# Layer 0's feed-forward spread between layer 1's attention steps, and two slot units of layer 3 begun in layer 2's scatter

## The chip, the cores and the metric

The kernel runs on one core of one Trainium2 chip. A core has five engines, each of which runs its own list of instructions in order: PE (matmuls and transposes), DVE (VectorE), ACT (ScalarE), POOL (GpSimd) and SP, which only issues DMAs here. An instruction waits until the semaphores that it names have been reached; what stands behind it on the same engine waits too. The metric is the time of one execution on the device, in microseconds. Before the change it is 901.73 us in the median of 14 runs (898.76 to 907.01).

## The reference

The input x is 16 sequences of 128 tokens of width 128, in float32. It goes through four layers; in each, a mixing step and a feed-forward add to x through a gate tanh(g). What matters here is this:

```python
x = x + tanh(g_xattn[0]) * L0_xattn(layernorm(x), ctx)      # 8 experts, each token goes to 2 of them, chosen by ctx
x = x + tanh(g_ffn[0])   * L0_ffn(layernorm(x))             # below
x = x + tanh(g_xattn[1]) * L1_xattn(layernorm(x), ctx, ctx) # 16 heads of 8, over blocks of 64 tokens
x = x + tanh(g_ffn[1])   * L1_ffn(layernorm(x))             # 8 linear maps, one chosen per output element
x = x + tanh(g_xattn[2]) * L2_xattn(..., hops)              # a gated memory; position rows picked by itok
x = x + tanh(g_ffn[2])   * L2_ffn(layernorm(x))             # experts choose tokens: gather, two products, scatter
x = x + tanh(g_xattn[3]) * L3_xattn(layernorm(x), ctx)      # slots: 3 rounds of attention and a GRU
x = x + tanh(g_ffn[3])   * L3_ffn(layernorm(x))             # weights rounded to -1, 0, 1

def L0_ffn(x):
    hq = float_quantize(relu(x @ w1.T + b1))                # 512 hidden, rounded to an 8-bit float
    return float_quantize(hq @ float_quantize(w2).T + float_quantize(b2))   # 16-bit float

def L3_xattn(slots, ctx):                                   # the slots are the 128 tokens of a sequence
    k, v = rmsnorm(ctx) @ Wk.T, rmsnorm(ctx) @ Wv.T
    for _ in range(3):
        attn = softmax(scale * (rmsnorm(slots) @ Wq.T) @ k.T, axis=slots)
        attn = attn / (attn.sum(over ctx) + eps)
        slots = gru(attn @ v, slots)
    return slots
```

The feed-forward of layer 0 and the norms work row by row, so each of the 16 sequences could go on by itself; layer 1's attention needs q from its own sequence alone, and k and v from ctx.

## The kernel before

x stays in on-chip memory as 16 tiles of 128 tokens by 128 (`k.x`). A "batch" is one such tile, a "chunk" four of them (BJ = 4, NJ = 4 chunks). The sub-layers are functions called in turn (`LAYERS`, L1721), and each is written as a pipeline over chunks, batches or blocks. What order an engine gets is set in two ways. In most sub-layers a planner orders the instructions, from its own estimate of durations and from what depends on what. In `l1_ffn`, `l2_ffn` and `l3_xattn`, `k.nc` is an `Engines` object (L51), which ties each instruction to the one before it on its engine (`InOrder`, L28), so that the order in the code is the order on the engine; this is called a told order.

*Layer 0.* `l0_xattn` (L284) sorts the tokens by expert into 39 blocks of 128 rows. A one-hot tile `of` serves to find the rows; then for each block GpSimd gathers the rows (`l_xs`, L454), SP loads the expert's first-layer weights (`l_w`, 258 KB each, into seven buffers in one tile of the tag w16a), PE computes, and the result goes to DRAM. `l0_returned(b)` (L503) brings the two expert outputs of each token of batch b back: two indirect DMAs on GpSimd (`l_back`, L512), each followed by an addition to x on VectorE (L519). Each gather is held behind the last addition but one (`k.behind`). `l0_ffn` (L545) issues the returns of chunk 0, then runs `pipeline(NJ, (hidden, 0), (output, 1))`: `hidden(j)` is the layer norm of chunk j (L197), four matmuls and relu into an 8-bit tile, and the two returns of a batch of the next chunk after each matmul; `output(j)` is 16 fp8 matmuls, the bias (L583) and the addition to x.

*Position gathers.* Layer 2 needs 65 gathers of position rows by indirect DMA on GpSimd (L961). They are spread: `k.gather(done)` issues the next one behind the instruction given. In layer 1's attention `maxima` and `normed` each issue one per batch. `turn_positions(n)` (L970) transposes four gathered tiles on PE and ACT copies them; six of these lie in `l0_ffn`, the others in `l1_ffn`.

*Layer 1's attention* (L595) is a pipeline over 16 batches with eight stages: queries, maxima, turned, weights, values, normed, output, projected. `project(j)` makes the norm, q and k of chunk j, and `project_values(j)` its v; `queries` calls project(0) first and project(j+1) at batch 4j+2. GpSimd masks q and k by head (L663, twice per batch) and the turned maxima (L703). PE's first product of batch b takes the masked k and is called kz(b) below.

*Layer 1's feed-forward* (L797) runs 64 small steps in a told order, with three of the next norms (`pieces`) in it.

*Layer 2's scatter and layer 3.* At the end of `l2_ffn`, 19 told steps (t in range(19)) scatter the 16 units' outputs back to x, and in them the layer norm and first root-mean-square norm of chunks 0 to 2 are made (`l3_first`, advanced by `more`). Layer 3's attention (L1466) has 12 units, 3 rounds by 4 chunks; its loop starts at t = 1 and unit u passes through the turn of its normed slots at t = u + 1 (g), scores and softmax at u + 2 (b), the weighted sum at u + 3 (c) and the gates' tanh and the new state at u + 4 (d). Chunk 3's first norms are advanced in t = 1 to 3.

Of the kernel before, what the change touches and what calls it, by code (L numbers as in the profile page):

```python
# [18 lines left out]
P = 128  # L19
# [31 lines left out]
class Engines:  # L51


    def __init__(self, tc, nc):
        self.nc = nc
        self.tensor, self.vector, self.scalar, self.gpsimd = (
            InOrder(tc, e) for e in (nc.tensor, nc.vector, nc.scalar, nc.gpsimd)
        )
# [5 lines left out]
class Kernel:  # L64
# [29 lines left out]
    def w2k(self, name):  # L94
        return self.work.tile([P, 512], F32, tag="w2k", name=name, bufs=13)
# [101 lines left out]
    def norm(self, j, keep=None, twice=False, pow=None):  # L197


        nc = self.nc  # L200
        st = self.sm([P, BJ, 6], "ln_st")
        mv = self.sm([P, BJ, 2], "ln_mv")
        for i in range(BJ):
            nc.vector.bn_stats(st[:, i, :], self.x[:, BJ * j + i, :])
            nc.vector.bn_aggr(mv[:, i, :], st[:, i, :])
        rs = self.sm([P, BJ], "ln_rs")
        if pow is None:
            self.rsqrt(rs, mv[:, :, 1], 1e-5)
        else:
            nc.vector.tensor_scalar(rs, mv[:, :, 1], 1e-5, None, ALU.add)  # L210
            nc.gpsimd.tensor_tensor(rs, rs, pow, ALU.pow)
        yield
        xn = keep if keep is not None else self.w2k("xn").rearrange("p (b d) -> p b d", b=BJ)
        for i in range(BJ):
            nc.vector.tensor_scalar(
                xn[:, i, :], self.x[:, BJ * j + i, :], mv[:, i, 0:1], rs[:, i : i + 1], ALU.subtract, ALU.mult
            )
# [75 lines left out]
def l0_xattn(k):  # L293
# [94 lines left out]
    of = k.work.tile([P, 2 * NB, 2, NBLK], BF16, tag="l0_of", name="l0_of", bufs=1)  # L388
# [117 lines left out]
def l0_returned(k, b):  # L506
# [3 lines left out]
    for i in range(2):  # L510
# [5 lines left out]
        if len(k.l0_added) > 1:  # L516
            k.behind(dma, k.l0_added[-2])
# [26 lines left out]
def l0_ffn(k):  # L544
# [11 lines left out]
    k.l0_added = []  # L556
    l2_gates_of_ctx(k)
    for b in range(BJ):
        l0_returned(k, b)

    def hidden(j):
        k.layernorm(j)
        hq = k.work.tile([P, NF, N], FP8, tag="w4k", name="l0f_q", bufs=3)
        for f in range(NF):
# [3 lines left out]
            if j + 1 < NJ:  # L568
                l0_returned(k, BJ * (j + 1) + f)
            if j and f % 2:  # L570
                turn_positions(k, 2 * (j - 1) + f // 2)
        return hq

    def output(j, hq):
# [7 lines left out]
        y = k.work.tile([P, N], F16, tag="w2k", name="l0f_y", bufs=13)  # L582
# [6 lines left out]
    pipeline(NJ, (hidden, 0), (output, 1))  # L589
# [3 lines left out]
def l1_xattn(k):  # L593
# [9 lines left out]
    k.banks(bank=8)  # L603
# [6 lines left out]
    nc.gpsimd.memset(neg, -1.0)  # L610
    for g in range(G):
        rows = neg[32 * g : 32 * g + 32, :]
        nc.gpsimd.affine_select(
            out=rows, in_=rows, pattern=[[-2, 4]], compare_op=ALU.is_ge, fill=0.0, base=0, channel_multiplier=1
        )
        nc.gpsimd.affine_select(
# [18 lines left out]
    for v in vs:  # L635
        nc.gpsimd.memset(v, 0.0)
        nc.gpsimd.memset(v[0:64, :, :, DH : DH + 1], 1.0)
        nc.gpsimd.memset(v[64:P, :, :, 2 * DH + 1 : 2 * DH + 2], 1.0)
    qkT = {}

    def project(j):
        k.layernorm(j)
# [27 lines left out]
    def queries(b):  # L670
        if b == 0:
            project(0)
            project_values(0)
        if b % BJ == 2 and b // BJ + 1 < NJ:
            project(b // BJ + 1)
        if b % BJ == 3 and b // BJ + 1 < NJ:

            project_values(b // BJ + 1)
        return masked(b)

    def maxima(b, qk):
# [11 lines left out]
        k.gather(done)  # L693
# [85 lines left out]
    for t in range(NB + 6):  # L779
        for fn, lag in stages:  # L780
            b = t - lag
            if 0 <= b < NB:
                args = (state.pop((after[fn], b)),) if fn in after else ()
                state[fn, b] = fn(b, *args)
        if t == NB + 1:

            xn = k.work.tile([P, BJ, P], F32, tag="w4k", name="l1f_xn", bufs=3)
            k.layernorm(0, keep=xn, pow=k.half)

def l1_ffn(k):
# [105 lines left out]
    for s in range(C * NJ + 24):  # L898
# [35 lines left out]
        if s % 2 and s // 2 <= P // 8 - 6:  # L934
            turn_positions(k, s // 2 + 6)
        for n in pieces.get(s, []):
            if n not in under_way:
                under_way[n] = k.norm(n[1], pow=k.half)
# [288 lines left out]
def l2_ffn(k):  # L1227
# [10 lines left out]
    k.l3_pool = k.l3_stack.enter_context(k.tc.tile_pool(name="l3_in", bufs=1, side="right"))  # L1238
    stack = ExitStack()
# [145 lines left out]
    k.l3_more = more  # L1385
    for t in range(NB + 3):
# [6 lines left out]
        more()  # L1393
        if t % BJ == 2 and t > 2:
# [71 lines left out]
def l3_xattn(k):  # L1466

# [54 lines left out]
    def weights(u, s, m):  # L1522
        rs = k.l3_rs[:, BJ * (u % NJ) : BJ * (u % NJ + 1)]
        tot, e = k.sm([P, BJ], "l3_tot"), w2k("l3_e")
# [7 lines left out]
    def weighted(u, tot):  # L1532
# [4 lines left out]
        v = pool.tile([P, BJ, P + 1], F32, tag="l3_vs", name="l3_vs")  # L1537
# [43 lines left out]
    sn, snT, at, ups, pg, sq = k.l3_first, {}, {}, {}, {}, {}  # L1581
    ffn = k.l3_ffn
    hs, norms = {}, {j: ffn.normed(j) for j in range(NJ)}
    for t in range(1, U + 4):
        a, g, b, c, d = (t - lag if 0 <= t - lag < U else None for lag in range(5))
        out = t - U - 1
        if t == NJ - 1:
# [29 lines left out]
        if t < NJ:  # L1617
# [98 lines left out]
LAYERS = [l0_xattn, l0_ffn, l1_xattn, l1_ffn, l2_xattn, l2_ffn, l3_xattn]  # L1716
# [86 lines left out]
```

## Time and profile before

| | us |
|---|---|
| median of 14 runs | 901.73 |
| profiled execution, its own time | 901.9 |
| span of the profiled execution | 900.2 |
| busy: PE / DVE / ACT / POOL | 728.2 / 515.4 / 402.0 / 421.5 |
| mean granted clock of PE | 0.909 |
| last block of layer 0's experts ends | 131.2 |
| feed-forward of layer 0, to its last fp8 matmul | 131.5 to 201.8 |
| layer 1's attention, first kz to the last stage | 210.28 to 340.87 |
| last norm's transposes in the scatter | 739.61 |

The profile is one execution. Its page gives the busy share of each engine in 40 slices of the span (22.5 us each; a digit is tenths), the chain of work that ended last, and groups of instructions. The trace behind it answers questions: a window's busy times, one line's instructions and whom they wait for, a chain of waits in a window. Lines of helpers stand for many callers: L112 is the matmul helper, L116 the transpose, L38 is every instruction in a told order, L215 the normalised x (`xn`). PE's times at half the granted clock are about twice those at full clock.

### The profile page before, as it was taken

Reading aid. Unit: us, or ns where it says so; the run is one execution under the profiler, and the core shown is the slowest. Engines: PE = TensorE matmul, PEld = TensorE weight load, DVE = VectorE, ACT = ScalarE, POOL = GpSimd, SP = SyncE. Lnnn points to the kernel's source line nnn. Section 1 sums busy time; section 2 is a strip of 40 time slices with the busy share of each in tenths; the row PEclk is TensorE's granted clock in tenths of the full one; section 3 lists DMA queues with packets and bytes.
Section 4 is the critical chain, followed back from the end, with each engine's and each line's share of the span. In section 5 each row is a group of like instructions: output and inputs, shape, how many; then the busy total and the mean of one; then the engine's idle time right before and its main releaser. Section 6 shows DMA issues by size and latency. Waiting matters only on the chain.

```text
span 900.2 us, 13278 instructions
## 1 busy us (share of the span) xinstructions
PE 728.2 (81%) x4349; PEld 487.8 (54%) x4349; DVE 515.4 (57%) x1462; ACT 402.0 (45%) x1006; POOL 421.5 (47%) x443
## 2 busy tenths in 40 slices
PE   3279981667897998998497899966899976999997
PEld 3179980333454564443297633335688964655555
DVE  6735543554555547879866136565711464777863
ACT  0035531233443455776126715522544443676552
POOL 6666645523655856776366405441300232555430
PEclk9989995876998999899869899985999996999999
DMA  8758851100000000000304113330000000000001
GB/s 252 209 133 222 205 140 38 41 27 4 19 16 19 26 22 18 0 1 0 93 1 126 30 48 94 95 128 2 1 1 0 1 2 0 1 1 1 1 1 47
DMA packets 43653, 46.49 MB, mean 52 GB/s; under 512 B 8368, under 2 KB 32560, under 8 KB 43456
## 3 DMA queue, kind: packets, MB, share of 16 engines
q1 hardware_dynamic: 37088, 35.63, 13.7%
q0 software_dynamic: 4384, 8.95, 4.3%
q10 hardware_dynamic: 2112, 1.05, 0.4%
q8 instruction: 35, 0.57, 0.3%
q14 instruction: 34, 0.28, 0.1%
HBM read 40.90 MB, written 4.72 MB: 51 GB/s over the span
## 4 chain that ended last, share of the span: by engine, by line
PE 51%; DVE 19%; POOL 7%; issue 6%; ACT 6%; DMA 4%; SPq 1%; ACTq 0%; POOLq 0%; DVEq 0%
PE ps_bank L112 16%; PE ps_bank L38 16%; PE ps_mm L112 12%; PE ps_acc L112 5%; POOL l_back L512 2%; DMA l_back<-l_out_d,l_rows 2%; DVE l_m L38 2%; PE ps_bank L116 1%; DVE l1f_r L38 1%; DMA l_cm<-l_gm_d 1%; POOL l_ss L1211 1%; ACT l_cm L1154 1%; DVE xn L38 1%; PE ps_tr L116 1%; DVE xnT L38 1%
## 5 line engine op out<-in xcount | busy, mean ns | idle before, releaser
L961 POOL DMA_INDIRECT pe<-in_L_xattn_rpe,itokT x65 | 64.4, 990 | 63.1 <-DVE l_top L690 20.7
L38 PE MATMUL ps_bank<-xnT,l1f_w 128*128 128x512 f32 x128 | 62.5, 618 | 0.4 <-ACT pe L38 0.4
L112 PE MATMUL ps_mm<-pe,ident 128*128 128x512 f32 x64 | 59.4, 1050 | 0.0
L690 DVE TENSOR_REDUCE l_top<-ps_bank 128x8 f32<-128x512 f32 x64 | 39.7, 683 | 33.9 <-PE ps_bank L112 33.9
L722 ACT ACTIVATE l_a<-ps_bank 128x512 f32<-128x512 f32 x64 | 33.2, 602 | 45.7 <-PE ps_bank L112 45.6
L484 DVE TENSOR_SCALAR l_h<-ps_mm,l_w 128x128 f32<-128x128 f32 x117 | 33.7, 344 | 33.0 <-ACT l_h L486 32.6
L1154 ACT ACTIVATE l_cm<-l_cm,l_g 128x128 f32<-128x128 f32 x128 | 39.3, 394 | 26.6 <-POOL l_cm L1147 26.6
L454 POOL DMA_INDIRECT l_xs<-l_rows_d,l_tok x39 | 37.1, 951 | 21.3 <-PE ps_acc L112 14.1
L112 PE MATMUL ps_acc<-l_w,l_h 128*128 128x128 f32 x312 | 45.6, 279 | 1.6 <-ACT l_w L471 1.3
L1147 POOL TENSOR_SCALAR_AFFINE_SELECT l_cm<-l_cm 128x512 f32<-128x512 f32 x32 | 23.6, 758 | 46.6 <-DMA l_cm<-l_gm_d 40.7
L112 PE MATMUL ps_mm<-l_xT,l_w 128*128 128x128 f32 x312 | 44.2, 279 | 0.4 <-ACT l_xT L469 0.4
L112 PE MATMUL ps_mm<-l_qz,pe 128*128 128x128 f32 x256 | 37.7, 314 | 6.7 <-ACT pe L1101 6.7
L512 POOL DMA_INDIRECT l_back<-l_out_d,l_rows x32 | 30.9, 967 | 25.9 <-DVE x L519 18.7
L112 PEld LDWEIGHTS ps_acc<-l_w,l_h 128*128 128x128 f32 x312 | 40.0, 193 | 2.6 <-ACT l_w L471 1.5
L1326 ACT ACTIVATE l2f_h<-ps_bank,sb_L_ffn_b1T 128x264 f32<-128x264 f32 x64 | 28.3, 481 | 28.3 <-PE ps_bank L112 28.3
L112 PEld LDWEIGHTS ps_mm<-l_xT,l_w 128*128 128x128 f32 x312 | 39.8, 196 | 0.6 <-ACT l_xT L469 0.6
L112 PEld LDWEIGHTS ps_mm<-l_qz,pe 128*128 128x128 f32 x256 | 36.1, 227 | 7.5 <-ACT pe L1101 7.5
L38 PEld LDWEIGHTS ps_bank<-xnT,l1f_w 128*128 128x128 f32 x128 | 24.1, 200 | 24.9 <-issue 17.3
L1335 DVE TENSOR_SCALAR l2f_y<-ps_bank,sb_L_ffn_b2T 128x264 f32<-128x264 f32 x16 | 7.9, 494 | 49.7 <-PE ps_bank L112 49.7
L38 POOL TENSOR_TENSOR ln_rs<-ln_rs,neg_half 128x4 f32<-128x4 f32 x14 | 14.7, 1051 | 45.1 <-DVE ln_rs L38 45.1
L38 PE MATMUL ps_bank<-xnT,sb_L_xattn_gru_whT 128*128 128x512 f32 x72 | 35.6, 604 | 0.0
L1211 POOL TENSOR_TENSOR l_ss<-l_ss,neg_half 128x16 f32<-128x16 f32 x8 | 23.3, 2914 | 26.3 <-DVE l_ss L1210 26.3
(422 smaller groups left out, 1965.3 us busy)
## 6 DMA issues: line engine op xcount, KB each, us to landing
l_w<-in_L_xattn_w1b SPq DMA_DIRECT2D x39, 258.0 KB
l_cm<-l_gm_d SPq DMA_DIRECT2D x64, 128.0 KB
l_out_d<-l_y SPq DMA_DIRECT2D x39, 64.0 KB
sb_L_xattn_W<-in_L_xattn_W SPq DMA_DIRECT2D x1, 2048.0 KB
sb_L_ffn_w<-in_L_ffn_w SPq DMA_DIRECT2D x1, 2048.0 KB
pe<-in_L_xattn_rpe,itokT POOLq DMA_INDIRECT x65, 2.6
x<-in_x ACTq DMA_DIRECT2D x4, 256.0 KB
ctxT<-in_ctxT SPq DMA_DIRECT2D x1, 1024.0 KB
```

Source lines behind the costliest of these rows:

```text
L38: done = op(*args, **kw)
L112: self.nc.tensor.matmul(out, lhsT, rhs, start=start, stop=stop)
L454: nc.gpsimd.indirect_dma_start(out=xs, out_offset=None, in_=rows_d, in_offset=bass.IndirectOffsetOnAxis(ap=tok[:, n : n + 1].bitcast(U32), ...
L484: nc.vector.tensor_scalar(h[:, cols], ph[:, cols], bias, 0.0, ALU.add, ALU.max)
L512: dma = nc.gpsimd.indirect_dma_start(out=y, out_offset=None, in_=k.l0_out_d, in_offset=bass.IndirectOffsetOnAxis(ap=k.l0_rows[:, 2 * b + i ...
L690: done = nc.vector.tensor_reduce(top[:, 32 * g : 32 * g + 8], ss[g].rearrange("p (n s) -> p n s", n=8), AX.X, ALU.max)
L722: nc.scalar.activation(a, ss[g], AF.Exp, scale=scale)
L961: dma = nc.gpsimd.indirect_dma_start(out=k.pe[:, g if g < G - 1 else P - 1, :], out_offset=None, in_=k.a["L2_xattn_rpe"], in_offset=bass.I ...
L1147: nc.gpsimd.affine_select(out=by_n(cm), in_=by_n(cm), pattern=[[0, 4], [1, P]], compare_op=ALU.is_ge, fill=1e30, base=0, channel_multiplie ...
L1154: nc.scalar.activation(part, part, AF.Exp, scale=-1.0, bias=g[:, n : n + 1])
L1211: nc.gpsimd.tensor_tensor(ss, ss, half, ALU.pow)
L1326: nc.scalar.activation(h, ph, AF.Gelu, bias=b1[:, e * NF + f : e * NF + f + 1])
```

## The change

`l0_ffn` no longer runs its pipeline: it returns `hidden` and `output`, and layer 1's attention calls them. In front remain 16 return gathers (batches 0 to 7) and seven turns of positions. The first step of attention calls the feed-forward of chunk 0 and then project(0). Steps t = 0 to 7 each issue the two returns of batch 8 + t, now without the hold behind an addition. At the end of step 4j `hidden(j+1)` is called, at the end of step 4j + 1 `output(j+1)`, and at 4j + 2 project(j+1). In all of this GpSimd's order is told, the other engines stay with the planner. The norms after the first take their inverse root from a power on GpSimd instead of ACT's root and VectorE's reciprocal. `maxima` issues a position gather only from batch 8 on, so eight of them move to layer 1's feed-forward. Two more 2 KB buffers are had by putting the one-hot tile `of` where the first expert weights go.

In layer 1's feed-forward the late norms' `xn` (three times four instructions) are computed on GpSimd. In layer 2's scatter the turn, scores, softmax and weighted v of layer 3's units 0 and 1 are advanced at t = 11, 13, 15 and 17; layer 3's loop starts at t = 3 without the scores of unit 1 (`b` is none there); chunk 3's norms are advanced twice in each of t = 3 and 4. Tiles that now live in the scatter come from a pool of their own (`early`; the renamed allocations are cut from the diff).

```diff
@@ -51,11 +51,10 @@
-    def __init__(self, tc, nc):
+    def __init__(self, tc, nc, names=("tensor", "vector", "scalar", "gpsimd")):
...
-        self.tensor, self.vector, self.scalar, self.gpsimd = (
-            InOrder(tc, e) for e in (nc.tensor, nc.vector, nc.scalar, nc.gpsimd)
-        )
+        for name in names:
+            setattr(self, name, InOrder(tc, getattr(nc, name)))
@@ -92,7 +91,7 @@
-        return self.work.tile([P, 512], F32, tag="w2k", name=name, bufs=13)
+        return self.work.tile([P, 512], F32, tag="w2k", name=name, bufs=15)
...
@@ -212,7 +212,7 @@
-            nc.vector.tensor_scalar(
+            (by or nc.vector).tensor_scalar(
@@ -385,7 +385,7 @@
-    of = k.work.tile([P, 2 * NB, 2, NBLK], BF16, tag="l0_of", name="l0_of", bufs=1)
+    of = k.wts.tile([P, 2 * NB, 2, NBLK], BF16, tag="w16a", name="l0_of")
@@ -513,7 +513,7 @@
             in_offset=bass.IndirectOffsetOnAxis(ap=k.l0_rows[:, 2 * b + i : 2 * b + i + 1].bitcast(U32), axis=0),
         )
-        if len(k.l0_added) > 1:
+        if len(k.l0_added) in range(2, 4 * BJ):
             k.behind(dma, k.l0_added[-2])
         k.l0_added.append(
@@ -554,21 +554,23 @@
     nc.vector.tensor_copy(bq, b2)
     k.l0_added = []
+    k.banks(bank=8)
+    k.nc = Engines(k.tc, k.nc, ("gpsimd",))
     l2_gates_of_ctx(k)
-    for b in range(BJ):
+    for b in range(2 * BJ):
         l0_returned(k, b)
+    for n in range(7):
+        turn_positions(k, n)
     def hidden(j):
-        k.layernorm(j)
+        k.layernorm(j, pow=k.half if j else None)
         hq = k.work.tile([P, NF, N], FP8, tag="w4k", name="l0f_q", bufs=3)
         for f in range(NF):
...
             k.mm(ph, w1[:, f * P : (f + 1) * P], k.chunk(k.xnT, j))
             nc.scalar.activation(hq[:, f, :], ph, AF.Relu, bias=b1[:, f : f + 1], saturate=False)
-            if j + 1 < NJ:
-                l0_returned(k, BJ * (j + 1) + f)
-            if j and f % 2:
-                turn_positions(k, 2 * (j - 1) + f // 2)
         return hq
@@ -579,18 +581,20 @@
-        y = k.work.tile([P, N], F16, tag="w2k", name="l0f_y", bufs=13)
+        y = k.work.tile([P, N], F16, tag="w2k", name="l0f_y", bufs=15)
...
-    pipeline(NJ, (hidden, 0), (output, 1))
-def l1_xattn(k):
+    return hidden, output
+def l1_xattn(k, ffn):
@@ -600,20 +604,19 @@
-    k.banks(bank=8)
...
-    nc.gpsimd.memset(neg, -1.0)
+    k.nc.nc.gpsimd.memset(neg, -1.0)
...
-        nc.gpsimd.affine_select(
+        k.nc.nc.gpsimd.affine_select(
...
-        nc.gpsimd.affine_select(
+        k.nc.nc.gpsimd.affine_select(
@@ -633,13 +636,13 @@
-        nc.gpsimd.memset(v, 0.0)
-        nc.gpsimd.memset(v[0:64, :, :, DH : DH + 1], 1.0)
-        nc.gpsimd.memset(v[64:P, :, :, 2 * DH + 1 : 2 * DH + 2], 1.0)
-    qkT = {}
+        k.nc.nc.gpsimd.memset(v, 0.0)
+        k.nc.nc.gpsimd.memset(v[0:64, :, :, DH : DH + 1], 1.0)
+        k.nc.nc.gpsimd.memset(v[64:P, :, :, 2 * DH + 1 : 2 * DH + 2], 1.0)
+    qkT, hq = {}, {}
...
-        k.layernorm(j)
+        k.layernorm(j, pow=k.half if j else None)
@@ -668,14 +671,16 @@
     def queries(b):
+        j, i = divmod(b, BJ)
         if b == 0:
+            ffn[1](0, ffn[0](0))
             project(0)
             project_values(0)
-        if b % BJ == 2 and b // BJ + 1 < NJ:
-            project(b // BJ + 1)
-        if b % BJ == 3 and b // BJ + 1 < NJ:
-            project_values(b // BJ + 1)
+        if i == 2 and j + 1 < NJ:
+            project(j + 1)
+        if i == 3 and j + 1 < NJ:
+            project_values(j + 1)
         return masked(b)
@@ -690,7 +695,8 @@
                 top[:, 32 * g : 32 * g + 8], ss[g].rearrange("p (n s) -> p n s", n=8), AX.X, ALU.max
             )
-        k.gather(done)
+        if b >= NB // 2:
+            k.gather(done)
         return qz, top
@@ -782,10 +788,19 @@
                 args = (state.pop((after[fn], b)),) if fn in after else ()
                 state[fn, b] = fn(b, *args)
+        j, i = divmod(t, BJ)
+        if t < 2 * BJ:
+            l0_returned(k, 2 * BJ + t)
+        if j + 1 < NJ:
+            if i == 0:
+                hq[0] = ffn[0](j + 1)
+            if i == 1:
+                ffn[1](j + 1, hq.pop(0))
         if t == NB + 1:
             xn = k.work.tile([P, BJ, P], F32, tag="w4k", name="l1f_xn", bufs=3)
             k.layernorm(0, keep=xn, pow=k.half)
+    k.nc = k.nc.nc
@@ -931,11 +946,11 @@
                 ):
                     fn(m, half)
-        if s % 2 and s // 2 <= P // 8 - 6:
-            turn_positions(k, s // 2 + 6)
+        if s % 2 and s // 2 <= P // 8 - 7:
+            turn_positions(k, s // 2 + 7)
         for n in pieces.get(s, []):
             if n not in under_way:
-                under_way[n] = k.norm(n[1], pow=k.half)
+                under_way[n] = k.norm(n[1], pow=k.half, by=nc.gpsimd if n[0] > C * NJ else None)
             next(under_way[n], None)
     k.nc = nc.nc
@@ -1236,6 +1251,7 @@
+    k.l3_early = k.l3_stack.enter_context(k.tc.tile_pool(name="l3_early", bufs=2, side="right"))
@@ -1383,6 +1399,9 @@
     k.l3_more = more
+    k.l3_units = l3_steps(k)
+    early = (11, 13, 15, 17)
     for t in range(NB + 3):
         if 0 <= t - 3 < NB:
@@ -1391,6 +1410,8 @@
             os[t + AHEAD - 1] = gated(t + AHEAD - 1)
         more()
+        if t in early:
+            next(k.l3_units)
         if t % BJ == 2 and t > 2:
             firsts[t // BJ - 1] = l3_first(k, t // BJ - 1)
@@ -1464,6 +1485,11 @@
+    for _ in k.l3_units:
+        pass
+def l3_steps(k):
@@ -1473,9 +1499,7 @@
-    stack = ExitStack()
-    pool = stack.enter_context(k.tc.tile_pool(name="l3", bufs=2, side="right"))
-    w2k = lambda name: pool.tile([P, N], F32, tag=name, name=name)
+    early = lambda name, width=N: k.l3_early.tile([P, width], F32, tag=name, name=name)
...
@@ -1579,12 +1603,29 @@
     sn, snT, at, ups, pg, sq = k.l3_first, {}, {}, {}, {}, {}
+    def begun(g):
+        pt = turn(sn.pop(g))
+        snT[g] = early("l3_snT")
+        nc.vector.tensor_copy(snT[g], pt)
+    for u in range(2):
+        begun(u)
+        yield
+        s = scores(u, snT.pop(u))
+        e, tot = weights(u, s, tops(u, s))
+        at[u] = e, weighted(u, tot)
+        yield
+    stack = ExitStack()
+    pool = stack.enter_context(k.tc.tile_pool(name="l3", bufs=2, side="right"))
+    w2k = lambda name: pool.tile([P, N], F32, tag=name, name=name)
     ffn = k.l3_ffn
     hs, norms = {}, {j: ffn.normed(j) for j in range(NJ)}
-    for t in range(1, U + 4):
+    for t in range(3, U + 4):
         a, g, b, c, d = (t - lag if 0 <= t - lag < U else None for lag in range(5))
+        b = None if t == 3 else b
         out = t - U - 1
-        if t == NJ - 1:
+        if t <= NJ:
             k.l3_more()
         if out >= 0:
@@ -1614,7 +1655,7 @@
             s = scores(b, snT.pop(b))
             m = tops(b, s)
-        if t < NJ:
+        if t <= NJ:
             k.l3_more()
         if c is not None:
@@ -1642,9 +1683,7 @@
-            pt = turn(sn.pop(g))
-            snT[g] = w2k("l3_snT")
-            nc.vector.tensor_copy(snT[g], pt)
+            begun(g)
@@ -1713,7 +1752,11 @@
-LAYERS = [l0_xattn, l0_ffn, l1_xattn, l1_ffn, l2_xattn, l2_ffn, l3_xattn]
+def l0_ffn_l1_xattn(k):
+    l1_xattn(k, l0_ffn(k))
+LAYERS = [l0_xattn, l0_ffn_l1_xattn, l1_ffn, l2_xattn, l2_ffn, l3_xattn]
```

More of the change, by code (lines that the diff above doesn't have):

```diff
@@ L195, in layernorm, with norm @@
                 return done.value
-    def norm(self, j, keep=None, twice=False, pow=None):
+    def norm(self, j, keep=None, twice=False, pow=None, by=None):
         nc = self.nc
@@ L1523, in weights @@
         rs = k.l3_rs[:, BJ * (u % NJ) : BJ * (u % NJ + 1)]
-        tot, e = k.sm([P, BJ], "l3_tot"), w2k("l3_e")
+        tot, e = k.sm([P, BJ], "l3_tot"), early("l3_e")
         for i in range(BJ):
@@ L1536, in weighted @@
         nc.gpsimd.tensor_tensor(tot, tot, k.l3_rs[:, BJ * j : BJ * (j + 1)], ALU.mult)
-        v = pool.tile([P, BJ, P + 1], F32, tag="l3_vs", name="l3_vs")
+        v = early("l3_vs", N + BJ).rearrange("p (b d) -> p b d", b=BJ)
         nc.gpsimd.tensor_tensor(
```

## The prediction

> **What bounds the kernel now.** I read the page's slices first, then the chain of waits, then windows over the stages that the change touches, then single queues.
>
> ```profile
> span 900.2 us, 13278 instructions
> PE   3279981667897998998497899966899976999997
> PEclk9989995876998999899869899985999996999999
> PE 51%; DVE 19%; POOL 7%; issue 6%; ACT 6%; DMA 4%; SPq 1%; ACTq 0%; POOLq 0%; DVEq 0%
> ```
>
> TensorE is busy in nearly every slice of 22.5 us. The soft places are slices 6 to 8 (layer 0's feed-forward, 131 to 203 us), and the seam before layer 3 near 750. The change goes at these two, and at a VectorE-bound tail near 430. The windows say what each stage holds; their columns are the window, its length, then busy time and instructions of PE, PE's weight loads, DVE, ACT and POOL, then granted clock, DMA share and GB/s:
>
> ```profile
> 131.50:203.00 71.50, 33.00 (x141) 19.14 (x141) 34.19 (x131) 18.25 (x32) 31.89 (x33) 0.69 0.15 42
> 210.30:341.00 130.70, 113.95 (x1125) 65.60 (x1126) 67.17 (x156) 57.30 (x129) 79.23 (x79) 0.93 0.07 18
> ```
>
> The feed-forward leaves PE idle for 38.5 of 71.5 us; attention leaves 16.7 of 130.7. So little idle time of PE is on offer to hide a feed-forward in. What the feed-forward waits for is seen in the answers on the gather line L512 and PE's timeline (start, duration, what; idle time before it and its releaser in brackets):
>
> ```profile
>   DVE x L519: 18.7, 22
> ...
> 165.30 0.33 PE L116 MATMUL ps_tr<-ident,xn 128*128 128x128 f32 x1 [2.90 <-DVE xn L215]
> 178.48 0.45 PE L116 MATMUL ps_tr<-ident,xn 128*128 128x128 f32 x1 [4.57 <-DVE xn L215]
> 193.21 0.45 PE L116 MATMUL ps_tr<-ident,xn 128*128 128x128 f32 x1 [5.62 <-DVE xn L215]
> ```
>
> GpSimd sat idle 18.7 us behind the adds that pace the 32 return gathers (1.63 us each), and PE waits for the norm of each chunk. From the last fp8 matmul to the first scores the chain is serial:
>
> ```profile
> 201.82 0.69 DVE l0f_y L583
> 202.51 0.27 DVE xn L215
> ...
> 202.91 1.08 PE ps_bank L116 x4
> ...
> 204.70 3.80 PE ps_bank L112 x4
> ...
> 209.18 1.05 POOL l_kz L663
> ...
> 210.28 1.29 PE ps_bank L112 x8
> ```
>
> Layer 3's seam is serial as well, a norm, scores, a table load and exponentials one behind another:
>
> ```profile
> 742.87 1.02 POOL l_ss L38
> ...
> 747.05 2.09 PE ps_bank L38 x8
> ...
> 750.13 1.28 ACT L38
> 751.42 1.87 ACT l_e L38 x8
> ...
> 754.96 5.40 PE ps_bank L38 x18
> ```
>
> **Part A, the feed-forward between attention steps.** Removed: the stage as one block. Only its chunk 0, and 16 of 32 return gathers, stay in front. Gather 16 is issued at 160.63 in the profile; with the usual 2.5 us to its add, chunk 0's output (its matmuls at 154.8 to 162.4 stay where they are) gets y (0.68), the x add (0.75) and statistics (2.4): the norm for project(0) is ready at 168.1, not 202.5. Transposes 1.1, q and k 3.8, values 1.0 and the mask 1.04 follow, so kz(0) could start near 176 against 210.28: 34 us earlier.
>
> In PE's order of the changed kernel, however, chunk 1's transposes and first-layer matmuls stand before kz(0). Chunk 1's returns are long in, but its xn stands on VectorE behind adds 17 and 18, whose gathers stand in GpSimd's told order behind qz and kz (176.05); its power (1.03, row of ln_rs) stands behind both gathers: these at 176.35 and 177.6, the adds till 180.5, xn 180.55. PE has nothing else in its order and idles 5.7 us, then does transposes and matmuls (6.4); kz(0) starts at 187.4.
>
> After that each chunk j = 1 to 3 has the same four pieces on PE: a wait before its norm's transposes, 6.1 us of transposes and matmuls (rows 4.53 and 4.57, plus 1.1 and a copy), 1.2 us of fp8 matmuls, and a wait between the fp8 matmuls and project(j), because y, x add, eight statistics, power and xn (0.68 + 0.75 + 2.4 + 1.03 + 0.3, gaps 0.5) form a chain with no other matmul in PE's order between: 5.7. Walking the told orders with the trace's durations, the waits are 5.7 and 5.8 (chunk 1), 7.0 and 5.7 (chunk 2, whose power stands behind mz(3) and gathers 25 and 26), 5.0 and 5.8 (chunk 3): 35.0 in sum, with work of 21.9. Of these 56.9, 12.1 lie before kz(0) and 5.5 replace waits that projections 1 to 3 have today (PE's waits for xn at L116 are 6.6 in 200 to 345, less 1.1 at 202.9). So attention ends at 187.4 + 130.6 + 39.3 = 357.3 if nothing of it overlaps. The step-by-step walk has kz(1), (4), (5), (8), (9) at 203, 232, 250, 279 and 297.5 (before 220.2, 235.1, 248.5, 268.6, 284.5) and the end at 352.7 against 340.87, since late stages of a batch run during the waits. Steps 5 to 7 are bound by GpSimd: three masks at 1.04 and three gathers at 0.97 to 1.25 are 6.9, where a step took 6.1. Taken: **+12**. Bounds: +17, nothing overlapped and 0.5 of clock; -13, all six waits hidden (357.3 - 35.0 = 322.3, and the 5.5 that were subtracted come back as the six do: 327.8). I take the walk, because every wait in it is a chain of rows.
>
> Eight matrices less of position gathers leave attention (0.97 each, GpSimd no bound there) and run in layer 1's feed-forward, where GpSimd is busy 27.8 of 50 us: +0.3 (0 to 1).
>
> The first-layer weights of layer 0 now share memory with the one-hot tile `of`, so their first seven loads (258 KB each, issued 34.6 to 38) wait until its matmuls end at 43.84. The first hidden matmul is at 50.0; the loads have 6 us with the DMA engines at 0.22. +0.5 (0 to 1.5).
>
> Costed at nothing: the seventh turn of positions in front (four transposes, 1.1 us, in PE's 38.5 idle us there); two more buffers of 2 KB and the banks set up earlier, which add no instruction; the power on GpSimd (1.03) for ACT's root and VectorE's reciprocal, which is in the walk; one turn less in layer 1's feed-forward, off the chain, since VectorE bounds it.
>
> **Part B, the late norms on GpSimd.** Layer 1's tail is bound by VectorE in the chain: the four xn at 424.59 (1.01), 435.84 (0.93) and 446.63 (1.03). GpSimd needs 0.49 to 0.61 for such a tile (L993, L994), 2.2 for four, in stretches where it is idle. -3 (-4 to -1; the lower gain if an add then waits for GpSimd's xn).
>
> **Part C, units 0 and 1 of layer 3 in the scatter.** The iterations t = 1 and 2 (741.2 to 754.96, 13.7 us) vanish. But PE gets units' turn, scores and waits inside the scatter (1.33 us a step, and PE already waited 2.27 at 731.13): scores of two units are 4.2 us of PE, the table load (1.28) and the exponentials come ahead of the scatter's next norm on ACT, and GpSimd's weighted product behind its power; I put 5 us there. Chunk 3's norm, once spread over t = 1 to 3, now lies in t = 3 and 4: 742.87 to 747.05 stays in the path, about 4. 13.7 - 5 - 4 leaves **-5** (-10, the scatter hides the units whole; 0, t = 3 waits as long as t = 1 and 2 did).
>
> **Sum:** 12 + 0.3 + 0.5 - 3 - 5 = +4.8. The profiled execution took 901.9 (span 900.2), which is the median of 901.73 within 0.2: 906.7, forecast 906.
>
> [...] The trace shows a granted clock of 0.50 in 206 to 210 (1.13 us idle before 202.91) and in 279 to 285 (2.78 idle before), and 0.50 from 747 for 13 us after 5.23 idle, then 1.00. [...]
>
> **Rivals.** (1) *The feed-forward hides after all* (the other side): the waits are filled because VectorE and GpSimd run ahead. For it: attention's PE waits today are short (6.6 and 3.3 us), so the engines do run ahead. Against: PE's order holds no other matmul there. All hidden would be 901.9 - 13 - 3 - 5 + 0.8 = 882; a third of the 35 hidden, 895. It decides once 7.5 us (4.8 + 2.7) of the 35 vanish. (2) *The seam gives nothing*: the units' reciprocals and copies in VectorE's order hold up the scatter's adds, and t = 3 waits for chunk 3 anyway: 906.7 + 5 = 912, with A at its bound 917. For it: 2.27 at 731.13. (3) *It cancels*: A at +8, C at -7: 901. For it: the walk's error is about 1 us in each of six waits.
>
> **How the numbers follow.** A measurement of this kernel tells 0.3% (2.7 us) from no change. Forecast as walked: 0.50, own range 901 to 912 (of it 0.40 slower, 0.10 within). Rival 1: 0.17, all faster. Rival 2: 0.20, slower. Rival 3: 0.13, of it 0.08 within, 0.05 faster. Together 0.22 faster, 0.18 within, 0.60 slower. The range goes from 891 (half of rival 1 outside) to 917 (the bound of A with rival 2).
>
> **What would show it.** First scores kz(0) near 187, PE waiting 5 to 7 us for xn six times from 175 to 292, kz(9) near 297, attention's end near 353; VectorE's xn gone from the tail; layer 3's matmul group of 754.96 some 5 us closer to the scatter's last norm (739.61) than today. The prediction fails if PE's waits for xn in that stretch come to under 25 us, or the scatter's 17 steps hold the units with no wait of over 1 us.

## The result and the profile after

The changed kernel takes 945.60 us in the median of 13 runs (943.18 to 950.89), the kernel before 904.46 (62 runs). The ratio is 1.0465, 95% interval 1.0445 to 1.0485: 41 us slower. The forecast was 906, with a range of 891 to 917. Its profiled execution has a span of 945.8 us, 45.6 over the profiled one of before. The page's head, slices and chain:

```profile
span 945.8 us, 13239 instructions
PE   2279993455586699878967779995779987999997
PEclk9999996668776799988996999997599998999999
PE 50%; DVE 20%; POOL 8%; issue 7%; DMA 6%; ACT 5%; ACTq 0%; SPq 0%; POOLq 0%; DVEq 0%
```

Counted from 0, as in the prediction, the feed-forward left three slices (6 to 8) with PE at 0.1 to 0.6. Now there are eight such slices (6 to 13), seven of them with PE at 0.3 to 0.6 and one at 0.8, and the granted clock in them is 0.6 to 0.8. The stages' ends say where the time went (the starts of the named instructions in the two traces):

| landmark | before | after | difference | of it new |
|---|---|---|---|---|
| last block of layer 0 (L496) | 131.18 | 131.62 | +0.4 | +0.4 |
| kz(0), the first scores | 210.28 | 191.86 | -18.4 | -18.9 |
| attention's last projection (L1_xattn_Wo) | 340.55 | 381.71 | +41.2 | +59.6 |
| last norm of layer 1's feed-forward | 450.62 | 503.37 | +52.8 | +11.6 |
| scatter's first norm | 722.54 | 775.01 | +52.5 | -0.3 |
| layer 3's first input-gate matmul | 763.42 | 808.72 | +45.3 | -7.2 |

So attention, started 18 us earlier, ends 41 us later, layer 1's feed-forward adds 11.6 that nobody had on the bill, and layer 3's seam gives 7.2 back. The windows of that stretch, before (2 lines) and after (2 lines), with the columns named in the prediction:

```profile
131.50:210.30 78.80, 39.49 (x160) 22.73 (x160) 38.06 (x145) 20.13 (x37) 34.04 (x36) 0.68 0.14 38
210.30:341.00 130.70, 113.95 (x1125) 65.60 (x1126) 67.17 (x156) 57.30 (x129) 79.23 (x79) 0.93 0.07 18
```

```profile
131.90:191.90 60.00, 30.19 (x120) 18.72 (x120) 19.29 (x64) 13.95 (x23) 24.36 (x29) 0.69 0.14 42
191.90:382.20 190.30, 135.03 (x1198) 76.53 (x1198) 92.68 (x232) 63.73 (x137) 88.63 (x88) 0.81 0.07 16
```

PE is busy for 165.2 us (30.19 + 135.03) where it was for 153.4: 11.8 us of the 41. Of these, 3.3 are matmuls for the gates of layer 2 (tile `l_gw`, 3.75 us against 0.44), which the kernel before ran mostly inside layer 0's experts; they lie ahead of chunk 0's norm, where PE idles. The other 8.5 are nearly the same matmuls (one turn of positions more) at a lower granted clock, 0.81 and not 0.93 in the second window. The other 29.0 of the 41 are idle time of PE (85.1 against 56.1). PE's waits in the trace after, 176 to 390 us, give in total, times and longest; then the same view of before, 203 to 345:

```profile
PE ps_bank L115 <- DVE xn L215: 39.1, 7, 7.7
PE ps_bank L115 <- DVE l_top L695: 9.6, 4, 4.2
PE ps_bank L111 <- DVE l_top L695: 5.4, 4, 2.9
```

```profile
PE ps_bank L116 <- DVE xn L215: 6.6, 4, 2.8
PE ps_bank L116 <- DVE l_top L690: 3.3, 2, 2.6
```

The waits for xn are those of the forecast. Those for l_top, the maxima, are new. The chain of waits after shows why VectorE is late with the maxima:

```profile
215.34 1.04 POOL l_mz L38
...
216.54 3.99 DMA l_back<-l_out_d,l_rows
...
220.56 0.51 DVE x L519
...
221.10 0.36 DVE x L519
...
221.78 0.59 DVE l_top L695
...
222.46 1.18 DVE l_top L695 x2
...
223.68 0.48 PE ps_bank L115
```

GpSimd issues the two returns of a step behind the mask mz in its told order; VectorE has the two additions ahead of the last maxima in its order and waits for the DMA; PE waits for the maxima. VectorE waited 26.7 us in 13 places for returns in 165 to 390. A second thing lengthens the additions themselves (timeline of VectorE, then of GpSimd):

```profile
180.83 3.23 DVE L519 SCALAR_TENSOR_TENSOR x<-l_back,l_w,x 128x128 f32<-128x128 f32 x2 [8.35 <-DMA l_back<-l_out_d,l_rows]
```

```profile
180.46 1.05 POOL L38 TENSOR_TENSOR ln_rs<-ln_rs,neg_half 128x4 f32<-128x4 f32 x1
181.50 1.03 POOL L38 TENSOR_TENSOR l_qz<-l_qT,mask8x 128x512 f32<-128x512 f32 x1
182.49 1.03 POOL L38 TENSOR_TENSOR l_kz<-l_kT,mask8x 128x512 f32<-128x512 f32 x1
```

Two additions of 0.35 took 3.23 us, until GpSimd's three instructions (the power and two masks) were done; the 32 additions are busy 19.9 us in all (mean 622 ns, page) where they had 349 each. In layer 1's feed-forward the same thing is larger (timelines of VectorE and of PE):

```profile
416.25 11.15 DVE L38 TENSOR_SCALAR xn<-x,ln_mv,ln_rs 128x128 f32<-128x128 f32 x4
```

```profile
428.05 1.11 PE L38 MATMUL ps_bank<-ident,xn 128*128 128x128 f32 x4 [8.62 <-DVE ps_bank L38]
```

One of the four xn is 10.38 us long there, while GpSimd works without a gap from 410.6 to 426.5, and PE idles 8.62 us behind it. Before, the four took 4.29 together:

```profile
374.07 4.29 DVE L38 TENSOR_SCALAR xn<-x,ln_mv,ln_rs 128x128 f32<-128x128 f32 x4
```

At layer 3's seam the gain is plain: the scatter's end runs into the recurrent matmuls, and one wait of 3.31 is left where 5.23 and 3.36 stood. Part of it is given back ahead of them, where the scatter's last norm now waits 3.17 instead of 1.18. PE before, then after:

```profile
739.61 1.10 PE L38 MATMUL ps_bank<-ident,xn 128*128 128x128 f32 x4 [1.18 <-DVE xn L38]
...
747.05 2.07 PE L38 MATMUL ps_bank<-l_snT,l_k 128*128 128x128 f32 x8 [5.23 <-DVE l_snT L38]
...
754.96 2.09 PE L38 MATMUL ps_bank<-l_vs,l_e 128*128 128x129 f32 x8 [3.36 <-ACT l_junk L38]
```

```profile
791.42 1.08 PE L38 MATMUL ps_bank<-ident,xn 128*128 128x128 f32 x4 [3.17 <-DVE xn L38]
...
799.85 1.88 PE L38 MATMUL ps_bank<-xnT,sb_L_xattn_gru_whT 128*128 128x512 f32 x4
805.04 1.11 PE L38 MATMUL ps_bank<-ident,l_up 128*128 128x128 f32 x4 [3.31 <-DVE l_up L38]
```

### The profile page after: what moved, and what is told of

It reads as the page before. It is cut to its first block, busy times and chain, and to the rows that moved or that the text cites. A ratio compares the mean times of both kernels' runs of the same rounds, so it can differ in the third digit from the quotient of the medians.

```text
span 945.8 us, 13239 instructions
## 1 busy us (share of the span) xinstructions
PE 732.3 (77%) x4349; PEld 486.1 (51%) x4349; DVE 523.6 (55%) x1444; ACT 400.8 (42%) x1000; POOL 441.2 (47%) x461
## 4 chain that ended last, share of the span: by engine, by line
PE 50%; DVE 20%; POOL 8%; issue 7%; DMA 6%; ACT 5%; ACTq 0%; SPq 0%; POOLq 0%; DVEq 0%
PE ps_bank L38 16%; PE ps_bank L111 15%; PE ps_mm L111 12%; PE ps_acc L111 5%; DMA l_back<-l_out_d,l_rows 3%; PE ps_bank L115 2%; DMA l_cm<-l_gm_d 2%; DVE xn L38 2%; POOL l_back L38 2%; DVE l_m L38 1%; POOL l_mz L38 1%; ACT l_cm L1169 1%; DVE l1f_r L38 1%; POOL l_ss L1226 1%; DVE xnT L38 1%
## 5 line engine op out<-in xcount | busy, mean ns | idle before, releaser
L38 PE MATMUL ps_bank<-xnT,l1f_w 128*128 128x512 f32 x128 | 64.8, 638 | 0.0
L115 PE MATMUL ps_bank<-ident,xn 128*128 128x128 f32 x36 | 10.8, 449 | 61.2 <-DVE xn L215 61.2
L1162 POOL TENSOR_SCALAR_AFFINE_SELECT l_cm<-l_cm 128x512 f32<-128x512 f32 x32 | 24.9, 798 | 44.9 <-PE ps_mm L111 32.7
L111 PE MATMUL ps_mm<-l_xT,l_w 128*128 128x128 f32 x312 | 44.5, 281 | 0.4 <-ACT l_xT L469 0.4
L519 DVE SCALAR_TENSOR_TENSOR x<-l_back,l_w,x 128x128 f32<-128x128 f32 x32 | 19.9, 622 | 44.9 <-DMA l_back<-l_out_d,l_rows 44.8
L111 PE MATMUL ps_mm<-l_qz,pe 128*128 128x128 f32 x256 | 34.0, 288 | 9.8 <-ACT pe L1116 9.8
L115 PEld LDWEIGHTS ps_bank<-ident,xn 128*128 128x128 f32 x36 | 6.5, 182 | 65.0 <-issue 46.5
L1342 ACT ACTIVATE l2f_h<-ps_bank,sb_L_ffn_b1T 128x264 f32<-128x264 f32 x64 | 28.1, 481 | 27.2 <-PE ps_bank L111 27.2
L38 POOL TENSOR_TENSOR ln_rs<-ln_rs,neg_half 128x4 f32<-128x4 f32 x21 | 22.1, 1052 | 34.9 <-DVE ln_rs L38 27.1
L38 PEld LDWEIGHTS ps_bank<-xnT,l1f_w 128*128 128x128 f32 x128 | 25.0, 208 | 25.3 <-issue 19.1
L111 PEld LDWEIGHTS ps_mm<-l_qz,pe 128*128 128x128 f32 x256 | 31.6, 200 | 11.4 <-ACT pe L1116 11.4
```

The source lines that it names most:

```text
L38: done = op(*args, **kw)
L111: self.nc.tensor.matmul(out, lhsT, rhs, start=start, stop=stop)
L115: self.nc.tensor.transpose(out, in_, self.ident[:n, :n])
L519: nc.vector.scalar_tensor_tensor(k.x[:, b, :], y, k.l0_w[:, b, i : i + 1], k.x[:, b, :], ALU.mult, ALU.add)
L1162: nc.gpsimd.affine_select(out=by_n(cm), in_=by_n(cm), pattern=[[0, 4], [1, P]], compare_op=ALU.is_ge, fill=1e30, base=0, channel_multiplie ...
L1342: nc.scalar.activation(h, ph, AF.Gelu, bias=b1[:, e * NF + f : e * NF + f + 1])
```

## The experiments

Each kernel was timed in turns with the kernel before on the same chip. Three kernels (the early norms on GpSimd, distance with free order, layer 3's part with the late norms) ran on a chip that takes 916.84 us for the kernel before, 12 more than the others (kz(0) comes 9.7 and 12.4 us later there in the two pairs of traces that can be compared); so each is compared by its difference to the kernel before on its own chip. The changed kernel stands at +41.1.

**Layer 3's units alone.** The kernel before with this part:

```diff
+        if t in early:
+            next(k.l3_units)
...
-    for t in range(1, U + 4):
+    for t in range(3, U + 4):
```

> The kernel before with the third part alone (units 0 and 1 begun in the scatter). In the changed kernel the seam from the scatter's first norm to layer 3's first input-gate matmuls shrank by 7.2 us (722.54 to 763.42 is 40.88, 775.01 to 808.72 is 33.71). Theory: this gain is the part's own and holds by itself: 901.7 - 7 = 895 (893 to 897). Rival (the forecast's second): the gain there belongs to the other parts' timing, and alone the units hold up the scatter: 900 to 903.

Measured: 898.83 against 904.49, -5.7; ratio 0.994 (0.9909 to 0.9971). The seam is 33.7 us long (723.67 to 757.37) as in the changed kernel. The gain is the part's own; the rival falls. (The expectation counted from 901.7; from 904.49 its range is 896 to 900.)

**The spread feed-forward alone.** The changed kernel without layer 3's part, and:

```diff
-                under_way[n] = k.norm(n[1], pow=k.half, by=nc.gpsimd if n[0] > C * NJ else None)
+                under_way[n] = k.norm(n[1], pow=k.half)
```

> The changed kernel without the third part and with the late norms back on VectorE, so the feed-forward between attention steps alone. Theory: the whole loss is here (41.2 us at attention's end, 9.5 more by layer 1's first y in its feed-forward), and the late norms on GpSimd cost 2.1: 945.6 + 7.2 - 2.1 = 951 (949 to 953). Rival: the late norms save 3 as forecast, and layer 1's feed-forward is longer for another reason: 945.6 + 7.2 + 3 = 956.

Measured: 956.10, +51.6. Attention ends at 382.88 and layer 1's feed-forward takes 123.1 us from there (121.7 with the norms on GpSimd). So the whole loss is in this part, as the theory has it, but its 2.1 for the norms has the wrong sign: they save 1.4 in these two profiles. With 7.2 for the seam that makes 8.6 of the 10.5 us between this kernel and the changed one; the rest is unassigned, and the interval of this ratio (1.0461 to 1.0620) is wide.

**The eight position gathers back in attention.**

```diff
-        if b >= NB // 2:
-            k.gather(done)
+        k.gather(done)
```

> The changed kernel with the eight position gathers of batches 0 to 7 back in attention. Theory: in layer 1's feed-forward they put GpSimd's products some 5 us later, into the time of the third norm, whose four xn then take 11.15 us on VectorE (4.29 before); back in attention they cost little, since GpSimd has idle time there: 945.6 - 9.5 + 1 = 937 (935 to 940), xn of the third norm near 4.3. Rival: the loss in layer 1's feed-forward comes from the late norms on GpSimd, and the gathers in attention lengthen steps that GpSimd paces by 8 x 0.97: 946 to 953.

Measured: 935.12, +30.6, so 10.5 less. Layer 1's feed-forward takes 110.0 us from attention's end to the last norm (110.1 before), and the third norm's xn are as before:

```profile
415.36 4.29 DVE L38 TENSOR_SCALAR xn<-x,ln_mv,ln_rs 128x128 f32<-128x128 f32 x4
```

Attention ends at 382.19, where it ended at 381.71. The gathers cost nothing in attention and 11 us where the change put them.

**The same from the other side.** The kernel before with `if b >= NB // 2:` ahead of that gather, and nothing else:

> The kernel before with one edit: the eight position gathers of batches 0 to 7 leave attention and run in layer 1's feed-forward, as in the changed kernel. The forecast priced this at +0.3 (0 to 1). Theory from the run with the gathers back: GpSimd falls behind there, its products run without a gap, one xn of the third norm takes some 10 us on VectorE, and the stage is 9 to 12 longer; attention gains at most 2: 8 to 11 us above the kernel before of the same chip. Rival: only together with the late norms and the later start is it that dear: 0 to 3 above.

Measured: 913.57 against 905.15, +8.4; ratio 1.0083 (1.0050 to 1.0115). The long xn is there, in a kernel without any of the rest (timelines of VectorE and of GpSimd):

```profile
375.70 11.14 DVE L38 TENSOR_SCALAR xn<-x,ln_mv,ln_rs 128x128 f32<-128x128 f32 x4
```

```profile
374.96 1.25 POOL L38 TENSOR_TENSOR l1f_e<-l1f_e 128x512 f32<-128x512 f32 x1
376.18 2.49 POOL L38 TENSOR_TENSOR pe<-pe,l1f_top 128x512 f32<-128x512 f32 x2
378.64 1.25 POOL L38 TENSOR_TENSOR l1f_e<-l1f_e 128x512 f32<-128x512 f32 x1
379.86 2.47 POOL L38 TENSOR_TENSOR pe<-pe,l1f_top 128x512 f32<-128x512 f32 x2
```

GpSimd's lines follow each other end to start (a line gives start and length): this is the run that VectorE sits out.

**The two early norms' xn on GpSimd as well.** The changed kernel with

```diff
-                under_way[n] = k.norm(n[1], pow=k.half, by=nc.gpsimd if n[0] > C * NJ else None)
+                under_way[n] = k.norm(n[1], pow=k.half, by=nc.gpsimd if n[0] else None)
```

> The changed kernel with the xn of the two early norms in layer 1's feed-forward on GpSimd as well, so that VectorE has no instruction there whose start GpSimd's run of products can hold up. In the changed kernel one such instruction took 10.38 us (0.335 alone), while GpSimd worked without a gap from 410.6 to 426.5, and PE waited 8.62 behind it. Theory that VectorE is held up by GpSimd's run: that instruction goes, GpSimd's queue grows by 3.2, and the 11.6 us that this stage lost shrink by 5 or more: 936 to 941. Rival: PE waits there because GpSimd is late with its products, whatever VectorE does: 944 to 950.

Measured: 954.10 against 916.84, +37.3, so 3.9 less than the changed kernel, and the stage takes 118.5 us (121.7). PE's wait of 8.62 is gone, and waits of 3.9 for GpSimd's xn stand in its place. This lies between the two expectations, and the interval of the ratio (1.0347 to 1.0436, that is 32 to 40 us) reaches into both: VectorE's long instruction held up the stage by some 3 us, and how much of the rest is its doing is not shown. The 8.4 us that remain against 110.1 hold GpSimd's own lateness and the 6.3 us of xn that it was given on top, which this run doesn't separate.

**Norms begun a step earlier.** In the changed kernel statistics, power and xn of a spread norm are issued one attention step ahead of the transposes and matmuls:

```diff
             if i == 0:
-                hq[0] = ffn[0](j + 1)
+                hq[0] = begun(j + 1)
             if i == 1:
-                ffn[1](j + 1, hq.pop(0))
+                hq[0] = ffn[0](j + 1, hq[0])
+            if i == 2:
+                ffn[1](j + 1, hq.pop(0))
+                hq[1] = begun(j + 1)
```

(`begun` takes the first two steps of the norm; project(j+1) finishes it at 4j+3.)

> The changed kernel with each spread norm (statistics, power, xn) begun one attention step ahead of its transposes and matmuls: hidden's norm at the end of step 4j and its matmuls at the end of 4j+1, output at the end of 4j+2 with the norm for the projection, the projection at 4j+3. Theory of the distance: PE waits because its order puts these matmuls right behind what they need; most of the 39.1 us of waits for xn goes, some 25 us: 920 (912 to 928). Rival, VectorE and GpSimd themselves are late (additions of 2.8 us while GpSimd computes, a told queue of gathers): at most 8 us go: 938 to 946.

Measured: 928.83, +24.3, 16.8 less. That is 0.8 above the theory's range and far from the rival's: the waits for xn went from 44.4 to 27.2 (165 to 390 us), and those for l_top rose from 15.0 to 19.9.

**A whole step between them.** begun(j+1) at the end of 4j-1, its matmuls at 4j, output and the projection's norm at 4j+1, the projection at 4j+3.

> One step ahead took 16.8 us off the changed kernel, but there the projection's transposes still stand right behind the fp8 matmuls in PE's order, and PE still waits 8.4, 7.2 and 6.3 us for their xn. Here hidden's norm is begun at the end of step 4j-1, its matmuls stand at the end of 4j, output and the projection's norm at the end of 4j+1, the projection at 4j+3, so a whole attention step lies between each of them. Theory of the distance: these three waits go as well, PE's waits for xn fall under 10 us and the clock stays up: 928.8 - 20 = 909 (904 to 914). Rival: VectorE's additions, which wait for GpSimd's gathers in the same steps, hold everything behind them, and the waits only change their name (l_top instead of xn): 920 to 929.

Measured: 916.65 against 905.67, +11.0 (ratio 1.0105, 1.0084 to 1.0127), 30 less than the changed kernel. The theory's number was missed by 8: attention ends at 351.7, and PE still waits 21.9 for xn and 10.8 for l_top. Its busy time from 132 to 352 is 159.6 (165.2 in the changed kernel), and the clock from kz(0) on is 0.87 (0.81): it came up as the waits went.

**Both: a whole step between, and the gathers back.**

> The same, and the eight position gathers back in attention, which took 10.5 us off the changed kernel. If the two are independent: 909 - 10.5 = 898 (893 to 904), near the kernel before with the third part alone (898.8). Rival: without the waits attention is paced by GpSimd (three masks and three gathers a step, 6.9 us by the forecast), and the gathers cost their 0.97 each: 904 to 910.

Measured: 906.93, +1.3 (ratio 1.0011, 0.9984 to 1.0038). The time lies in the rival's range, but the gathers did not cost: they are worth 9.7 here too, so the two are independent, and the start from 916.65 instead of 909 makes up the miss.

**All returns in front.** The same with `for b in range(NB): l0_returned(k, b)` ahead of attention, in the told order.

> The same as the run with two steps and the gathers back, and all 32 return gathers in front of attention, so that no addition waits for a gather between the steps. Theory that additions in VectorE's order hold up the maxima (PE waited 15 us for l_top in the changed kernel, 3.3 before): the waits for l_top go back to about 3 us and steps get shorter by 10 or more, but the gathers 17 to 32 end some 26 us later (1.63 each) than the 16 in front, of which chunk 0's matmuls cover about 12: in sum 0 to +8 against that run. Rival: the additions cost nothing there, and it is 14 us or more slower.

Measured: 913.28, +7.6, so 6.3 more than the run before it, within 0 to +8. kz(0) starts at 202.9 instead of 184.7, and attention from there to its last projection takes 155.6 us instead of 167.2. But PE's waits for l_top did not go (14.9 against 11.1), so the shortening is not in the waits that the theory named. It is in those for xn, which from kz(0) to the end of attention fall from 18.9 us in seven places to 7.4 in two. Whether the returns made the xn late through the additions in VectorE's order or through the power behind the gathers in GpSimd's, the run doesn't separate. And the maxima can be late without any addition: in this run PE waits 4.92 us for one of them until 217.38, and the transposes of four xn follow it at 217.65 without a wait, so these xn were ready by then. In the changed kernel four such xn take 2.31 us from 202.26 on, while GpSimd computes two masks, and 1.11 at 183.98, when it is idle.

**GpSimd's order left to the planner.** One edit in the changed kernel:

```diff
-    k.nc = Engines(k.tc, k.nc, ("gpsimd",))
+    k.nc = Engines(k.tc, k.nc, ())
```

> The changed kernel with GpSimd's order in the stage left to the planner. If the told order is what makes the power and the masks late behind the gathers (chunks 1 and 2 by 2 to 3 us each): 945.6 - 5 = 940 (935 to 943). Rival, the waits are chains of dependences and the order on GpSimd matters little: 943 to 948. If the planner puts gathers ahead of masks: over 948.

Measured: 920.63 against 905.67, +15.0: 26 less than the changed kernel, five times what any theory gave it. The planner issues 15 of the last 16 returns one behind another from 164.87 to 183.95, beside chunk 0 and project(0), and the last one behind the first four masks, and still starts kz(0) at 190.2. The end of this in the timeline of GpSimd, and the waits of PE (165 to 380 us):

```profile
183.95 0.95 POOL L512 DMA_INDIRECT l_back<-l_out_d,l_rows  x1 [0.30 <-DVE xn L215]
184.92 1.06 POOL L666 TENSOR_TENSOR l_qz<-l_qT,mask8x 128x512 f32<-128x512 f32 x1
...
189.11 0.98 POOL L512 DMA_INDIRECT l_back<-l_out_d,l_rows  x1 [0.16 <-DVE x L519]
```

```profile
PE ps_bank L115 <- DVE xn L215: 34.4, 9, 10.4
...
PE ps_bank L115 <- DVE l_top L695: 3.6, 2, 2.9
```

Attention ends at 355.9 (381.7): the waits for l_top are nearly gone, those for xn from kz(0) on are 22.9 us (32.1), the clock from 190 to 356 is 0.86, PE is busy for 157.8 us and idle for 66.6 (165.2 and 85.1 in the changed kernel). What the told order put into attention's steps cost 18.5 us of idle time and 7.4 of busy time.

**Distance and free order together, gathers back.**

> The run with two steps' distance and the gathers back (906.9), with GpSimd's order in that stage left to the planner, which alone took 25 us off the changed kernel: it issues the last 16 return gathers beside chunk 0, before kz(0), and attention's steps lose two gathers, two additions and the waits for them. Theory: distance and queue are separate losses in part; VectorE still waits 25 us for returns within attention there, half of it on PE's path: 906.9 - 12 = 895 (889 to 900). Rival: they are the same waits seen from two sides, and distance has taken them already: 903 to 909.

Measured: 910.41 against 916.84, -6.4; ratio 0.9933 (0.9910 to 0.9957). That is 7.7 below the told variant, at the small end of the theory's range (7 to 18 less than that run). It beats both kernels, but see the next run.

**Layer 3's part and the late norms on GpSimd, the feed-forward in one block.**

> The third part and the late norms on GpSimd, without the spread feed-forward. Theory from the stages of the runs so far (121.7 us with the late norms on GpSimd, 123.1 on VectorE, other things equal; 110.0 against 110.1 in another pair): the norms save 0 to 1.5, so 898.8 - 0.7 = 898 (896.5 to 899). Rival, the forecast's 3 us: 896 or less.

Measured: 911.04 against 916.84, -5.8; ratio 0.9930 (0.9904 to 0.9956), against -5.7 for layer 3's part alone. The norms save nothing that can be told. And the spread feed-forward, mended in three ways, is level with the feed-forward in one block: its whole gain is layer 3's.

## Why the prediction was wrong

Its direction held, its size did not: the sum was +4.8, the profiled executions differ by 45.6.

- **The start.** kz(0) was put at 187.4 and came at 191.86. Chunk 0's matmuls took 6.65 instead of 5.96, the two additions ahead of chunk 1's xn 3.23 instead of 0.7, and chunk 1's matmuls 5.64 instead of 4.57.
- **The six waits.** Forecast 5.7, 5.8, 7.0, 5.7, 5.0, 5.8, sum 35.0; measured 7.0, 6.8, 7.7, 7.3, 3.9, 6.4, sum 39.1. This step was right, and putting a whole step between norm and matmuls took 30 us off, as it should if they are chains of dependences.
- **The step that failed: the walk of the attention steps between the waits** ("+12 ... I take the walk, because every wait in it is a chain of rows"). From kz(0) to attention's end it had 165.3 us (187.4 to 352.7); measured are 190.2 (191.86 to 382.0), 24.9 more. The walk saw the additions ahead of xn, not ahead of the maxima, and took them at 0.35. They made VectorE late for PE, and GpSimd's told order made them late: 15.0 us of waits for l_top where 3.3 stood, which is 11.7 of the 24.9. The waits for xn in this stretch add 2.8 (32.1 for 29.3), and the first-layer matmuls of chunks 2 and 3 4.2 (next point). The 6.2 that remain are near the 4.6 that the walk took off for late stages running during the waits (357.3 to 352.7) and 1.6 more of attention's own products, but no run isolates them. Leaving GpSimd's order to the planner brought attention's end to 355.9, near the walk's 352.7, though with other terms: the first-layer matmuls were as slow there (6.45 and 6.00 us) and the waits for xn shorter.
- **The clock.** The walk took the durations of the rows of before, 4.5 us for a chunk's first-layer matmuls (4.57 and 4.53, at a granted clock of 0.79 in both). That term was too small. Behind waits of 7.0, 7.7 and 3.9 us these took 5.64, 6.66 and 6.65, at granted clocks of 0.65, 0.55 and 0.55; over the four chunks they take 25.6 us where they took 19.1:

```profile
242.28 6.66 PE L111 MATMUL ps_bank<-xnT,sb_L_ffn_w1T 128*128 128x512 f32 x8 [0.68 <-ACT xnT L106]
...
300.32 6.65 PE L111 MATMUL ps_bank<-xnT,sb_L_ffn_w1T 128*128 128x512 f32 x8 [0.68 <-ACT xnT L106]
```

  Attention's own products came out slow in places (kz(3) at 224.09 took 2.09 at a granted clock of 0.50, after 4.17 idle, where kz(0) took 1.14 at 1.00), but in sum they made only 1.6 (117.2 for 115.6). No run shows the 0.5 of clock in the forecast's upper bound: in its place the runs show the 8.5 us by which the busy time of the same matmuls grew. Which of the waits went with which drop of the clock, no run separates.
- **The moved gathers, priced at +0.3 (0 to 1).** Measured +8.4 alone, 10.5 and 9.7 taken back in two other kernels. The reason given, that GpSimd was busy only 27.8 of 50 us, was an average over 400 to 450; the gathers fall at 384 to 409, just ahead of a run of products in which GpSimd has no idle time at all.
- **The late norms, -3.** 0.1 in the pair of runs that isolates them, 1.4 in the other. GpSimd needs 3.15 to 3.8 for the four, not 2.2.
- **The first-layer weights, +0.5.** Right: the seven loads are issued from 44.5 on, the first hidden matmul is 2.8 later, and the loop ends 0.4 later.
- **Layer 3's seam, -5 (-10 to 0).** Right: -7.2 in the profile, -5.7 in the runs with it alone.
- **The rivals.** The first (the feed-forward hides) was the opposite of what came; even the mended kernels (+1.3, and -6.4 with the order left to the planner, both with layer 3's 5.7 in them) stay far from its 882 with all waits hidden, 20 us below the kernel before, and the latter of them comes near its 895, with a third hidden. The second rival was refuted by the run with layer 3's part alone. None held a longer layer 1.

What stays open: why the xn wait out GpSimd's run (11.1 to 11.2 us for the four in all six kernels that move the gathers and leave these xn on VectorE), while in all seven kernels with the gathers in attention the four take 4.3, in the kernel before inside a run as dense (368.40 to 384.4) with none over 1.31.

## What to carry to other kernels

Work that is moved between the steps of a tight pipeline must be walked on every engine that it touches, and for each of its instructions one asks what stands behind it in that engine's order: here two small additions a step, ahead of the maxima, brought 11.7 us of waits that nobody had counted. Put a full step between a chain's links (norm, matmul, output, next norm), and issue transfers while the front of the stage is busy with something else, not in the steps; that they must lie beside other work, and not ahead of it, is seen in the told run with all of them in front, which was 6.3 us slower. An average of free time over a stage says nothing on a queue in it; look at the stretch in which the moved instructions will land.

## What the runs showed of the hardware

In the changed kernel some of VectorE's additions and normalisations took longer while GpSimd computed: 0.35 (the median of 32) became up to 2.85 us for an addition, and 0.335 became 10.38 for a normalisation, over some eight of GpSimd's products; in the kernel before, four such normalisations took 0.61 to 1.31 each beside the same products. The long one ended at 426.63, GpSimd's run at 426.54; by what VectorE was held there, no run shows. The maxima, which read PE's results (`ps_bank`), kept their 0.68 throughout (0.658 to 0.692 over all 64).
